# Turning the experts' rows in a mixture-of-experts stage: TensorE transposes against DMA transposes of 16-bit halves

## The chip, the cores and the metric

The kernel runs on one core of a Trainium2 chip. The metric is the device time of one execution in microseconds; the median of the runs is used. The profile comes from one more execution, taken by the hardware profiler. PE is TensorE (matrix products; PEld is its weight load), ACT is ScalarE, DVE is VectorE, POOL is GpSimd and SP is SyncE, which here only issues DMAs.

## The reference

Four steps run one after the other on 2048 tokens (8 x 256) of width 256: an attention by autocorrelation, a feed-forward step with eight experts of 256 tokens each, a cross attention with 16 heads, and a mixture of experts with two experts for each token beside a shared expert. Each step reads the layer norm of `x` and is added to it. The change touches the last step:

```python
x = x + _L1_ffn_ref(_layernorm(x, axis=-1), gate_W, w1_e, w3_e, w2_e, w1_s, w3_s, w2_s)

def _L1_ffn_ref(hidden_states, gate_W, w1_e, w3_e, w2_e, w1_s, w3_s, w2_s):
    flat = hidden_states.reshape(-1, d)
    probs = jax.nn.softmax((flat @ gate_W.T).astype(jnp.float32), axis=-1)
    top_v, top_i = jax.lax.top_k(probs, 2)
    gates = jnp.zeros((T, e), probs.dtype).at[jnp.arange(T)[:, None], top_i].set(top_v)
    g = jax.nn.silu(jnp.einsum('td,edf->etf', flat, w1_e))
    u = jnp.einsum('td,edf->etf', flat, w3_e)
    out_e = jnp.einsum('etf,efd->etd', g * u, w2_e)
    routed = jnp.einsum('te,etd->td', gates, out_e)
    ...   # shared: the same form with w1_s, w3_s, w2_s
    return 0.5 * shared + 0.5 * routed
```

Everything is float32, with inner width F = 1024 and E = 8 experts.

## The kernel before

**The sparse form.** Only the chosen pairs of token and expert are computed. The router writes each token's row (256 normed values, eight gates, the token's number: ROW = 265 floats) into a buffer `Td` in memory, where every expert has its own range. `load_rows(e)` (L3489) reads an expert's first 512 rows into the tile `R`, [128, 4, 265], by one DMA on SyncE's queue (530 KB); there is one such buffer. The few rows beyond 512 are handled in 32-row slots by the generator `slots()` (L3598), a step at a time beside the blocks, with its own weight loads (`sab`, `sc`, L3593).

**Turning.** Products need the model width on the partitions, but `R` has the tokens there. `Turned` (L3497) turns the rows: `half(kc)` makes four TensorE transposes of 128x128 into a PSUM tile `pt` (L3509) and one ScalarE copy of the 512 columns to `RT` (L3512). The first half also copies the token numbers and gates out of `R` (L3514, L3515, VectorE). Two halves make an expert's `RT`, [128, 2, 512].

**Blocks and units.** The stage's main part is a loop over NBLK = 11 blocks b of 512 rows each: 0 and 1 for the shared expert, 2 to 9 for the eight experts, 10 for the shared expert again. A block is four up units (b, 0) to (b, 3), each giving 2 x 128 of the 1024 inner columns of both w1 and w3, and one down unit. The down unit of block b - 1 stands between (b, 0) and (b, 1). Each unit computes its 2x2 block product with seven partial products in place of eight. Sums of operands are formed ahead by VectorE: `UpWeights.steps` (L3105) for the weights, into `HP`, `DownWeights.steps` (L3134) into rows of `X`, `Rows.steps` (L3159) for the turned rows, into `T` and `RT`. All of these sums are lines L3083, which is a helper.

**The order inside a unit** is written out by hand in `run_unit` (L3407), and engines work in the order in which it emits:

```python
u.mm(u.a, A11, "b11", True); u.seed()            # ACT copies a to B
if before is not None: before.silu_2()           # ACT, previous unit
u.mm(u.e, S1, "t1", True);   u.read_p5()         # ACT reads e
end_open()                                       # previous unit's last product, gate, sums
for do in early: do()
u.mm(u.a, S2, "t2");         u.read_u2()         # ACT reads a
u.mm(u.b, A12, "b21")
for do in amid: do()
u.mm(u.e, S4, "b22");        u.read_c12()        # DVE
for do in late: do()
u.mm(u.a, S3, "t3");         u.read_c22()        # DVE
for do in after: do()
```

`seed` is L3222, `read_p5` L3245 and `read_u2` L3249. In a down unit `read_u2` is two scaled copies to the output rows `Y` (L3353). PSUM tiles `a` and `e` come in pairs; S2 writes over the `a` that seed reads, and S3 over the `a` that `read_u2` reads. The products of up units are L3234, those of down units L3293. In the lists `early`, `amid`, `late` and `after` the block loop (L3796) puts side work. The two halves of an expert's turning go to `early` and `amid` of the down unit in the block before the expert's own, its row sums to `late`. For the first expert they go to unit (1, 3), with the sums after it.

**SyncE's queue.** DMAs are issued in program order; one that waits holds back all behind it. In a block these are the next expert's `wab` (2 x 1 MB, after (b, 0), L2916), `R` (after the down unit), `wc` (1 MB, after (b, 1), L2926), and, in blocks 3 to 6, the slots' `sab` and `sc`, emitted in (b, 3). `Od` in memory collects the output; GpSimd adds each expert's rows to it by scattering DMAs (`add_rows`, L3517).

`HP` (16 x 265 floats for each partition) held the routed rows earlier; in this part its first 3072 floats hold weight sums. `X` holds the residual; its rows 0 to 5 are reused for the down weights' sums, and its last four rows lie in `Od` until block 10 fetches them back.

Of the kernel before, what the change touches and what calls it, by code (L numbers as in the profile page):

```python
# [8 lines left out]

F32 = mybir.dt.float32  # L10
BF16 = mybir.dt.bfloat16
U32 = mybir.dt.uint32
I32 = mybir.dt.int32
AF = mybir.ActivationFunctionType
ALU = mybir.AluOpType
# [4 lines left out]
P = 128  # L20
LN_EPS = 1e-5
CAP1 = 576
FIRST = 512
# [1063 lines left out]
def fast_path(  # L1087
# [33 lines left out]
    nc = tc.nc  # L1121
    B, S, D = x.shape
    T = B * S
    NT = T // P
    KC = D // P
    TPB = S // P
    E = L0_ffn_w1.shape[0]
# [22 lines left out]
    X = res.tile([P, NT, D], F32, name="X")  # L1150
# [3 lines left out]
    ROW = D + E + 1  # L1154
# [13 lines left out]
    ident = const.tile([P, P], F32, name="ident")  # L1168
# [93 lines left out]
    pm = l0.enter_context(tc.tile_pool(name="pm", bufs=2))  # L1262
# [34 lines left out]
    for dst, src, i in (  # L1297
# [12 lines left out]
        out=bqd.rearrange("o (b c) -> (o b) c", b=B),  # L1310
        in_=L0_xattn_bq.partition_broadcast(B),
    )
    nc.scalar.dma_start(
        out=WZ[:, :, DH : 2 * DH],
        in_=L0_xattn_Wq.rearrange("(kc p) c -> p kc c", p=P),
# [267 lines left out]
    for h in range(TPB):  # L1583
# [36 lines left out]
        out=tri,  # L1620
        in_=tri,
# [26 lines left out]
    for sign, base in ((1, 1), (-1, 16)):  # L1648
        nc.gpsimd.affine_select(
            out=rows_f,  # L1650
            in_=rows_f,
# [33 lines left out]
    for r in range(2):  # L1685
        (nc.sync if r == 0 else nc.scalar).dma_start(
            out=Gd[0, 0 : S * W2].rearrange(
                "(tt p r w) -> p tt r w", p=P, r=2, w=S
            )[:, :, r, :],
            in_=G,  # L1690
# [4 lines left out]
        out=DG,  # L1695
        in_=Gd[0, :].rearrange("(tt p w) -> p tt w", p=P, w=W2 + 1)[:, :, 1 : S + 1],
# [53 lines left out]
    for tt in range(2):  # L1750
# [3 lines left out]
    rest = pa.tile([P, S], F32, name="rest")  # L1754
# [4 lines left out]
        out=rest, in_to_replace=top[:, 0, :], in_values=pcorr, imm_value=-3.0e38  # L1759
# [16 lines left out]
        out=Wd[:, 0:W2].rearrange("o (r s) -> o r s", r=2),  # L1776
        in_=wrow.unsqueeze(1).to_broadcast([P, 2, S]),
# [4 lines left out]
        out=CW,  # L1782
        in_=bass.AP(wd.tensor, wd.offset + P - 1, [[WD - 1, P], [P, 2], [1, S]]),
# [186 lines left out]
    sums = pa.tile([P, NT, 2], F32, name="sums")  # L1970
# [50 lines left out]
    halves = [slice(m * S, (m + 1) * S) for m in range(2)]  # L2021
# [7 lines left out]
    b = order_b  # L2029
# [101 lines left out]
    def load_row(e):  # L2131
# [14 lines left out]
        out=Yd.rearrange("(c p) d -> p c d", p=P),  # L2146
        in_=blank[:, 0:D].unsqueeze(1).to_broadcast([P, NT, D]),
# [300 lines left out]
    for e in range(E - 1):  # L2448
        if e == 5:

            wpv = L1_xattn_Wp.rearrange("(c g m d) n -> m g d c n", c=NB, g=4, m=2)
            for m in range(2):
                for g in range(4):
# [3 lines left out]
                        out=bvc[r0 : r0 + DH, :],  # L2457
                        in_=bkv[:, 1, :].rearrange("(c g m) d -> m g d c", c=NB, g=4)[m, g],
# [70 lines left out]
    ps_m = banks.enter_context(tc.tile_pool(name="ps_m", bufs=3, space=PSUM))  # L2529
# [436 lines left out]
    for b in range(B):  # L2966
        for c in range(NB):
# [55 lines left out]
            if prev is None:  # L3023
# [12 lines left out]
                HP = pg1.tile([P, NT, ROW], F32, name="HP")  # L3036
# [20 lines left out]
    FULL = FIRST // P  # L3057
# [7 lines left out]
    lrows = slice(LAST * (TB // P), NT)  # L3065
    HT2 = TB // 2
    HF = F // 2
# [17 lines left out]
    class UpWeights:  # L3085


        def __init__(self, wab, sums, s1=None):
            self.sums = sums
            self.raw = {  # L3090
                (h, kc): wab[:, :, kc, h * HF : (h + 1) * HF]
                for h in range(2)
                for kc in range(KC)
            }
            self.part = {
                A11: self.raw[0, 0],
                A12: self.raw[0, 1],
                A22: self.raw[1, 1],
                S1: self.raw[1, 0] if s1 is None else s1,
                S3: sums[:, :, 0],  # L3100
                S2: sums[:, :, 1],
                S4: sums[:, :, 2],
            }
# [120 lines left out]
    class Up(Unit):  # L3224
        n = TB
# [56 lines left out]
    class Down(Unit):  # L3282
        n = HT2
# [123 lines left out]
    def run_unit(u, early=(), amid=(), late=(), after=()):  # L3407

        before = open_unit[0]
        u.mm(u.a, A11, "b11", True)  # L3410
        u.seed()
        if before is not None:
            before.silu_2()
        u.mm(u.e, S1, "t1", True)
        u.read_p5()
        end_open()
        for do in early:
            do()
        u.mm(u.a, S2, "t2")
        u.read_u2()  # L3420
        u.mm(u.b, A12, "b21")
        for do in amid:
            do()
        u.mm(u.e, S4, "b22")
        u.read_c12()
        for do in late:
            do()
        u.mm(u.a, S3, "t3")
        u.read_c22()
        for do in after:  # L3430
            do()
        open_unit[0] = u
# [56 lines left out]
    def load_rows(e):  # L3489
        R = pe2.tile([P, FULL, ROW], F32, tag="R", name="R", bufs=1)  # L3490
        nc.sync.dma_start(
            out=R,
            in_=Td[e * CAP1 : e * CAP1 + FIRST, :].rearrange("(r p) w -> p r w", p=P),
        )
        return R

    class Turned:  # L3497


        def __init__(self, e, R):  # L3500
            self.e, self.R = e, R
            self.RT = pe2.tile([P, KC, FIRST], F32, tag="RT", name="RT")
            self.ids = pe2.tile([P, FULL], U32, tag="ids", name="ids", bufs=3)
            self.gates = pe2.tile([P, FULL], F32, tag="gts", name="gts", bufs=3)

        def half(self, kc):
            pt = ps_m.tile([P, FULL, P], F32, tag="pm", name="pt")
            for r in range(FULL):
                nc.tensor.transpose(  # L3509
                    pt[:, r, :], self.R[:, r, kc * P : (kc + 1) * P], ident  # L3510
                )
            nc.scalar.copy(self.RT[:, kc, :], pt.rearrange("p r q -> p (r q)"))  # L3512
            if kc == 0:
                nc.vector.tensor_copy(self.ids, self.R[:, :, ROW - 1])  # L3514
                nc.vector.tensor_copy(self.gates, self.R[:, :, D + self.e])  # L3515

    def add_rows(Y, ids):  # L3517
        nc.gpsimd.indirect_dma_start(  # L3518
# [164 lines left out]
    pe2 = ctx.enter_context(tc.tile_pool(name="pe2", bufs=2))  # L3683
# [63 lines left out]
    ps_m = ctx.enter_context(tc.tile_pool(name="ps_m", bufs=1, space=PSUM))  # L3747
# [23 lines left out]
    turned = {}  # L3771

    def up_unit(b, k):
        u = Up(ups[b], xs_[b], k, acts.setdefault(b, []))
        u.with_sums = b < NBLK - 1
        return u

    def down_unit(b):
        if b < 2:
            return SharedDown(downs[b], acts.pop(b), b + 1)  # L3780
        t = turned.pop(b)
        return RoutedDown(downs[b], acts.pop(b), t.gates, t.ids)
# [13 lines left out]
    for b in range(NBLK):  # L3796


        n = b + 1
        rest = ups[b].steps(P, HF) if b >= 2 else []  # L3800
        run_unit(up_unit(b, 0), after=rest[:2])
        if b == 0:
            Rs[2] = load_rows(0)
        if b >= 2 and b - 1 < E:
            W_up[b - 1] = load_up(w1p, b - 1)
        halves = []
        if 2 <= n < NBLK - 1:
            t = turned[n] = Turned(n - 2, Rs.pop(n))
            xs_[n] = Rows(t.RT)
            halves = [lambda: t.half(0), lambda: t.half(1)]  # L3810
        sums = xs_[n].steps() if n < NBLK else []
        if b > 0:
            late = b == 1
            run_unit(
                down_unit(b - 1),
                early=([] if late else halves[:1]) + rest[2:],
                amid=[] if late else halves[1:],
                late=[] if late else sums,
            )
        if 2 <= b < E:  # L3820
            Rs[b + 2] = load_rows(b)
        for k in range(1, NK):
            early, amid, after = [], [], []
            if k == 1 and 2 <= n < NBLK:
                ups[n] = UpWeights(WS[0] if n == NBLK - 1 else W_up.pop(n - 2), SW)
                after = ups[n].steps(0, P)
            if 2 <= b < NBLK - 1:
                if k == 2:
                    downs[b] = DownWeights(W_down.pop(b - 2), TW)
                    after = downs[b].steps()[:2]  # L3830
                if k == 3:
                    after = downs[b].steps()[2:]
            if b == 0:
                after = ([assign_slots], sums, shared_down.steps())[k - 1]
            if b == 1 and k == 3:
                early, amid, after = halves[:1], halves[1:], sums
            run_unit(up_unit(b, k), early, amid, after=after)
            if k == 1:
                if b >= 2 and b - 1 < E:
                    W_down[b - 1] = load_down(w1p, b - 1)  # L3840
                if b == 1:
                    flags()
                    experts = slot_experts()
                if b == 2:
                    beside = slots()
                if b == NBLK - 1:
                    nc.sync.dma_start(out=X[:, lrows, :], in_=odv[:, lrows, :])
                    nc.sync.dma_start(
                        out=out.rearrange("b s d -> (b s) d")[0 : LAST * TB, :],
                        in_=Od[0 : LAST * TB, :],  # L3850
                    )
            if beside is not None and (b, k) != (2, 2):
                next(beside, None)
        if b == 1:
            Rs[3] = load_rows(1)
    last_down(WS[1], acts.pop(NBLK - 1))
    order.close()

# [51 lines left out]
```

## Time and profile before

| | |
|---|---|
| median of 3 runs | 832.65 us (831.88 to 832.73) |
| the profiled execution | 830.43 us, of it 828.7 us from first to last instruction |
| granted TensorE clock | 0.998 |
| transposes of the experts' rows (L3509) | 64, from 452.3 to 711.7 us |
| their copies on ScalarE (L3512) | 16, 585 ns each |
| one steady block | 41.0 us |
| TensorE busy from 430 to 828 us | 392.4 of 398 us |
| ScalarE busy from 430 to 828 us | 143.4 of 398 us |

The page of a profile lists, in parts, each engine's busy time, the span in slices, the DMA queues, the chain of work that ended last, the costliest groups of instructions and the DMA issues. In a group's line stand the source line, engine, operation, output and inputs, shapes and count; then busy us, mean ns of one, and the engine's idle time ahead of them with what ended it. In the timeline a line gives the start in us, the duration from the first start to the last end, engine, line, operation and how many were merged; a bracket is idle time before it and what it waited for. "SPq" is SyncE's queue.

### The profile page before, as it was taken

The page shows a single profiled execution, that of the slowest core. Times are in us where ns is not written, and L with a number is a line of the kernel's source. Part 1 is how long each engine was busy: PE and PEld are TensorE (multiplying, and loading weights), DVE is VectorE, ACT ScalarE, POOL GpSimd, SP SyncE. Part 2 cuts the span into 40 slices and gives each one's busy share as a digit, 9 for nine tenths or more (in the row PEclk, how much of TensorE's full clock was granted, in tenths as well). Part 3 has the DMA queues.
Part 4 walks back from the last instruction along what each step waited for, and adds up shares of the span by engine and source line. Part 5 has one row for each costly group of instructions (what it writes and reads, how often), then busy time and mean ns, then how long its engine had stood idle before and what let it go on. Part 6 is the DMA issues. An engine that isn't in the chain of part 4 may idle for free.

```text
span 828.7 us, 13872 instructions
## 1 busy us (share of the span) xinstructions
PE 806.3 (97%) x5188; PEld 636.2 (77%) x5188; DVE 522.3 (63%) x1470; ACT 348.7 (42%) x720; POOL 216.8 (26%) x293
## 2 busy tenths in 40 slices
PE   7999999999999999999999999999999999999997
PEld 6546787778745555557898989797979798999996
DVE  6377877440456586555775866767676758586731
ACT  4344454324377777431333233333333433443430
POOL 6251131230125455452330000202111232112020
PEclk9999999999999999999999999999999999999999
DMA  8395567942160000042120474656575754311023
GB/s 261 97 277 177 178 207 224 297 158 84 51 178 15 14 1 28 34 168 89 67 67 26 142 242 135 190 168 187 172 199 161 201 167 122 105 13 20 8 35 124
DMA packets 87316, 105.40 MB, mean 127 GB/s; under 512 B 9000, under 2 KB 77832, under 8 KB 87208
## 3 DMA queue, kind: packets, MB, share of 16 engines
q1 hardware_dynamic: 78568, 91.10, 35.0%
q0 software_dynamic: 7920, 13.02, 7.2%
q8 instruction: 43, 0.70, 0.4%
q10 hardware_dynamic: 752, 0.30, 0.1%
q14 instruction: 33, 0.27, 0.1%
HBM read 80.61 MB, written 25.37 MB: 128 GB/s over the span
## 4 chain that ended last, share of the span: by engine, by line
PE 88%; DMA 5%; DVE 3%; POOL 2%; ACT 1%; issue 1%; ACTq 0%; SPq 0%; DVEq 0%; POOLq 0%
PE a L3234 18%; PE e L3234 9%; PE a L3293 9%; PE py L2389 6%; PE ph L2372 5%; PE B L3234 5%; PE e L3293 4%; PE p L2652 4%; PE py L3439 3%; PE pv L2667 3%; PE B L3293 2%; PE pp L2718 2%; DMA R<-NMd,ids 2%; PE pgt L3196 2%; PE pp L2619 2%; PE pu L3196 2%
## 5 line engine op out<-in xcount | busy, mean ns | idle before, releaser
L3518 POOL DMA_INDIRECT Od<-Y,ids x32 | 51.6, 1612 | 300.5 <-DVE T L3083 184.0
L3222 ACT COPY B<-a 128x512 f32<-128x512 f32 (+1 forms) x54 | 28.6, 531 | 180.5 <-PE a L3234 142.6
L2660 ACT ACTIVATE ex<-p,scale 128x512 f32<-128x512 f32 x128 | 77.2, 689 | 27.5 <-PE p L2652 26.3
L3234 PE MATMUL a<-T,HP 128*128 128x256 f32 x288 | 73.9, 379 | 0.0
L3083 DVE TENSOR_TENSOR cc<-e,s 128x512 f32<-128x512 f32 x44 | 30.4, 691 | 58.0 <-PE e L3234 58.0
L3234 PE MATMUL a<-RT,wab 128*128 128x256 f32 x256 | 66.6, 383 | 0.0
L3083 DVE TENSOR_TENSOR act<-act 128x256 f32<-128x256 f32 (+1 forms) x120 | 61.4, 512 | 2.7
L2372 PE MATMUL ph<-RT,w 128*128 128x256 f32 x256 | 61.7, 389 | 0.8 <-ACT RT L2359 0.7
L2389 PE MATMUL py<-w,A 128*128 128x256 f32 x256 | 61.6, 388 | 0.0
L3234 PEld LDWEIGHTS a<-T,HP 128*128 128x128 f32 x288 | 54.0, 190 | 7.0
L3234 PEld LDWEIGHTS a<-RT,wab 128*128 128x128 f32 x256 | 46.4, 190 | 8.4 <-issue 1.6
L2381 ACT ACTIVATE A<-ph,b1c 128x256 f32<-128x256 f32 x64 | 30.0, 472 | 53.9 <-PE ph L2372 50.6
L2372 PEld LDWEIGHTS ph<-RT,w 128*128 128x128 f32 x256 | 45.3, 190 | 8.9 <-ACT A L2381 1.1
L2389 PEld LDWEIGHTS py<-w,A 128*128 128x128 f32 x256 | 46.6, 190 | 6.4
L2892 POOL DMA_INDIRECT Td<-HP,to x32 | 32.9, 1030 | 56.9 <-DMA Td<-HP,to 51.6
L2652 PE MATMUL p<-QM,KT 32*128 32x512 f32 x256 | 43.4, 640 | 0.4 <-DVE QM L2633 0.4
L3083 DVE TENSOR_TENSOR act<-act,cc 128x512 f32<-128x512 f32 x44 | 30.4, 691 | 17.6 <-ACT act L3268 17.1
L2399 POOL DMA_INDIRECT Yd<-Y,ids x16 | 15.7, 984 | 81.9 <-DVE Y L2398 49.0
L2667 PE MATMUL pv<-ex,VA 128*32 128x256 f32 x512 | 34.5, 385 | 0.2 <-DVE ov L2677 0.2
L3249 ACT COPY s<-a 128x512 f32<-128x512 f32 x44 | 25.7, 585 | 20.4 <-PE a L3234 20.4
L2667 PEld LDWEIGHTS pv<-ex,VA 128*32 128x32 f32 x512 | 13.5, 109 | 27.0 <-issue 11.7
L3234 PE MATMUL e<-T,wab 128*128 128x256 f32 x128 | 33.0, 380 | 0.3 <-DVE T L3083 0.3
(525 smaller groups left out, 1745.0 us busy)
## 6 DMA issues: line engine op xcount, KB each, us to landing
w<-in_L_ffn_w_dram SPq DMA_DIRECT2D x16, 1024.0 KB, 6.0
wab<-in_L_ffn_w_e_dram SPq DMA_DIRECT2D x16, 1024.0 KB, 4.9
wc<-in_L_ffn_w_e_dram SPq DMA_DIRECT2D x8, 1024.0 KB, 5.4
sab<-in_L_ffn_w_e_dram SPq DMA_DIRECT2D x32, 256.0 KB, 2.9
R<-Td SPq DMA_DIRECT2D x8, 530.0 KB, 3.7
sc<-in_L_ffn_w_e_dram SPq DMA_DIRECT2D x16, 256.0 KB, 2.8
Td<-blank SPq DMA_DIRECT2D x2, 1590.0 KB, 10.2
X<-in_x_dram SPq DMA_DIRECT2D x4, 512.0 KB, 5.3
```

Of the source, the lines that this page charges most:

```text
L2372: nc.tensor.matmul(ph, w1[:, kc, f * P : (f + 1) * P], RT[:, kc, :], start=(kc == 0), stop=(kc == KC - 1),)
L2381: nc.scalar.activation(A[:, f, :], ph, AF.Gelu_apprx_tanh, bias=b1c[:, e, f : f + 1])
L2389: nc.tensor.matmul(py, A[:, f, r * P : (r + 1) * P], w2[:, f, :], start=(f == 0), stop=(f == NF - 1),)
L2652: nc.tensor.matmul(ps[g].rearrange("p m q -> p (m q)"), KT[rows, c, k0 : k0 + P], QM[b][rows, c].rearrange("p m q -> p (m q)"), start=True ...
L2660: nc.scalar.activation(e4[:, g], ps[g], AF.Exp, scale=scale)
L2667: nc.tensor.matmul(pvs[b, c][32 * g : 32 * g + 32, m, :], VA[:, b * TPB + kt, 8 * c + 2 * g + m, :], ex[b, c, kt][:, g, m, :], start=(kt = ...
L2892: nc.gpsimd.indirect_dma_start(out=Td, out_offset=bass.IndirectOffsetOnAxis(ap=to[g][:, k, j : j + 1], axis=0), in_=HP[:, GT * g + j, :], ...
L3083: eng.tensor_tensor(out, a, b, op)
L3196: nc.tensor.matmul(ps, wab[:, m, kc, fs], xs[kc], start=(kc == 0), stop=(kc == KC - 1),)
L3234: nc.tensor.matmul(ps[:, m * HT2 : (m + 1) * HT2], self.w.get(m, left, self.k), self.x.part[right], start=start and m == 0, stop=True, ski ...
L3293: nc.tensor.matmul(ps[:, qs], self.acts[k][:, left, qs], self.w.get(right, k), start=start and i == 0 and k == 0, stop=(k == NK - 1), skip ...
L3518: nc.gpsimd.indirect_dma_start(out=Od, out_offset=bass.IndirectOffsetOnAxis(ap=ids, axis=0), in_=Y, in_offset=None, compute_op=ALU.add,)
```

## The change

The experts' rows are turned by DMA. A float32 is taken as two 16-bit halves, since the DMA transpose that is used moves 16-bit elements. `take_apart(i)` (ScalarE, two of the four groups of rows) copies the halves of `R` apart into a part of `X` that is idle then, low halves first, and issues two DMA transposes on SyncE's queue, of [128, 512] 16-bit elements each, into the unused end of `HP`. `join(kc)` (ScalarE) puts two turned halves together again into `RT`. The copies are of 16-bit integers, so the bits arrive unchanged.

Token numbers and gates are copied when `Turned` is made; their buffers are four in place of three. For expert b (of block b + 2), `take_apart` stands in `amid` of unit (b, 3), two blocks ahead of use, and `join` in `early` of the down unit in the block ahead. The first expert's `take_apart` stands in (1, 1), its `join` in (1, 3); the second's in (2, 0) and (2, 1), its sums in `late` of (2, 2). `load_rows(1)` moves from the end of block 1 to (1, 1).

```diff
     class Turned:
         def __init__(self, e, R):
-            self.e, self.R = e, R
+            self.ids = pe2.tile([P, FULL], U32, tag="ids", name="ids", bufs=4)
+            self.gates = pe2.tile([P, FULL], F32, tag="gts", name="gts", bufs=4)
+            nc.vector.tensor_copy(self.ids, R[:, :, ROW - 1])
+            nc.vector.tensor_copy(self.gates, R[:, :, D + e])
+            self.R = R
             self.RT = pe2.tile([P, KC, FIRST], F32, tag="RT", name="RT")
-            self.ids = pe2.tile([P, FULL], U32, tag="ids", name="ids", bufs=3)
-            self.gates = pe2.tile([P, FULL], F32, tag="gts", name="gts", bufs=3)
-
-        def half(self, kc):
-            pt = ps_m.tile([P, FULL, P], F32, tag="pm", name="pt")
-            for r in range(FULL):
-                nc.tensor.transpose(
-                    pt[:, r, :], self.R[:, r, kc * P : (kc + 1) * P], ident
-                )
-            nc.scalar.copy(self.RT[:, kc, :], pt.rearrange("p r q -> p (r q)"))
-            if kc == 0:
-                nc.vector.tensor_copy(self.ids, self.R[:, :, ROW - 1])
-                nc.vector.tensor_copy(self.gates, self.R[:, :, D + self.e])
+            self.parts = X[:, lrows, :].bitcast(U16)
+            self.turned = (
+                HP.rearrange("p n r -> p (n r)")[:, 2 * 3 * HF : 2 * 3 * HF + KC * FIRST]
+                .bitcast(U16)
+                .rearrange("p (c q) -> p c q", q=FIRST)
+            )
+
+        def take_apart(self, i):
+            two = slice(2 * i, 2 * i + 2)
+            nc.scalar.copy(
+                self.parts[:, two].rearrange("p r (t d) -> p r t d", t=2),
+                self.R[:, two, 0:D].bitcast(U16).rearrange("p r (d t) -> p r t d", t=2),
+            )
+            for r in (2 * i, 2 * i + 1):
+                nc.sync.dma_start_transpose(
+                    out=self.turned[:, :, r * P : (r + 1) * P],
+                    in_=self.parts[:, r],
+                )
+
+        def join(self, kc):
+            nc.scalar.copy(
+                self.RT[:, kc, :].bitcast(U16).rearrange("p (q t) -> p q t", t=2),
+                self.turned[:, kc : kc + 3 : 2, :].rearrange("p t q -> p q t"),
+            )
...
-        run_unit(up_unit(b, 0), after=rest[:2])
+        amid = []
+        if b == 2:
+            t = turned[n] = Turned(n - 2, Rs.pop(n))
+            amid = [lambda: t.take_apart(0), lambda: t.take_apart(1)]
+        run_unit(up_unit(b, 0), amid=amid, after=rest[:2])
...
-        halves = []
+        joins = []
         if 2 <= n < NBLK - 1:
-            t = turned[n] = Turned(n - 2, Rs.pop(n))
-            xs_[n] = Rows(t.RT)
-            halves = [lambda: t.half(0), lambda: t.half(1)]
-        sums = xs_[n].steps() if n < NBLK else []
+            t = turned[n] if n > 2 else None
+            if n > 3:
+                joins = [lambda: t.join(0), lambda: t.join(1)]
+                xs_[n] = Rows(t.RT)
+        sums = xs_[n].steps() if n in xs_ else []
         if b > 0:
-            late = b == 1
-            run_unit(
-                down_unit(b - 1),
-                early=([] if late else halves[:1]) + rest[2:],
-                amid=[] if late else halves[1:],
-                late=[] if late else sums,
-            )
+            run_unit(down_unit(b - 1), early=rest[2:] + joins, late=sums)
...
+            if b == 1 and k == 1 or 2 <= b < E and k == 3:
+                m = n if k == 1 else n + 1
+                v = turned[m] = Turned(m - 2, Rs.pop(m))
+                amid = [lambda: v.take_apart(0), lambda: v.take_apart(1)]
             if b == 1 and k == 3:
-                early, amid, after = halves[:1], halves[1:], sums
-            run_unit(up_unit(b, k), early, amid, after=after)
+                t = turned[n]
+                early, amid = [lambda: t.join(0)], [lambda: t.join(1)]
+                xs_[n] = Rows(t.RT)
+                after = xs_[n].steps()
+            if b == 2 and k == 1:
+                amid = [lambda: t.join(0), lambda: t.join(1)]
+                xs_[n] = Rows(t.RT)
+            if b == 2 and k == 2:
+                late = xs_[n].steps()
+            run_unit(up_unit(b, k), early, amid, late, after)
+            if b == 1 and k == 1:
+                Rs[3] = load_rows(1)
...
-        if b == 1:
-            Rs[3] = load_rows(1)
```

More of the change, by code (lines that the diff above doesn't have):

```diff
@@ L11 @@
 BF16 = mybir.dt.bfloat16
-U32 = mybir.dt.uint32
+U32, U16 = mybir.dt.uint32, mybir.dt.uint16
 I32 = mybir.dt.int32
@@ L3822, in fast_path @@
         for k in range(1, NK):
-            early, amid, after = [], [], []
+            early, amid, late, after = [], [], [], []
             if k == 1 and 2 <= n < NBLK:
```

## The prediction

> **What bounds the kernel now.** I read the page first: busy times, then the chain that ended last.
>
> ```profile
> PE 806.3 (97%) x5188; PEld 636.2 (77%) x5188; DVE 522.3 (63%) x1470; ACT 348.7 (42%) x720; POOL 216.8 (26%) x293
> PE 88%; DMA 5%; DVE 3%; POOL 2%; ACT 1%; issue 1%; ACTq 0%; SPq 0%; DVEq 0%; POOLq 0%
> ```
>
> TensorE is busy 97% of the span and is 88% of the chain; ScalarE has more than half its time free. So an instruction taken from TensorE shortens the run by what it occupies there, if nothing takes the gap. Second, the groups of instructions by shape, for the transposes that go and their copies:
>
> ```profile
> L3509 PE MATMUL pt<-ident,R 128*128 128x128 f32 x64 | 9.6, 273 | 0.0
> L3512 ACT COPY RT<-pt 128x512 f32<-128x512 f32 x16 | 9.4, 585 | 14.1 <-PE pt L3509 13.7
> ```
>
> 273 ns is one transpose from start to end; they are pipelined, so it isn't its price. Third, the timeline of TensorE around one group:
>
> ```profile
> 589.93 1.95 PE L3293 MATMUL B<-wc,act 128*128 128x128 f32 x16
> 591.72 0.60 PE L3509 MATMUL pt<-ident,R 128*128 128x128 f32 x4
> 592.16 1.95 PE L3293 MATMUL e<-wc,act 128*128 128x128 f32 x16
> ```
>
> Sixteen products take 1.79 us from start to start (589.93 to 591.72). The four transposes hold the next group back by 592.16 - 591.72 = 0.44 us, 110 ns each, and no line shows an idle bracket. The other fifteen groups give 0.43 or 0.44 us too. Fourth, ScalarE in the unit before the down unit of the same block, and then in that down unit:
>
> ```profile
> 572.79 0.41 ACT L3259 ACTIVATE act<-a 128x256 f32<-128x256 f32 x1
> 573.64 0.58 ACT L3249 COPY s<-a 128x512 f32<-128x512 f32 x1 [0.44 <-PE a L3234]
> 578.29 0.57 ACT L3222 COPY B<-a 128x512 f32<-128x512 f32 x1 [4.07 <-PE a L3234]
> 587.91 0.38 ACT L3259 ACTIVATE act<-a 128x256 f32<-128x256 f32 x1 [0.24 <-PE a L3234]
> 588.35 0.58 ACT L3512 COPY RT<-pt 128x512 f32<-128x512 f32 x1
> 590.13 0.62 ACT L3353 ACTIVATE Y<-a,gts 128x128 f32<-128x128 f32 x2 [1.20 <-PE a L3293]
> ```
>
> After read_u2 (L3249) ScalarE waits 4.07 us for the next unit's first product; elsewhere in the stage this gap is 2.87 to 3.1 us. Last, SyncE's queue over one block, where the weight loads are issued:
>
> ```profile
> 563.75 4.66 SPq L3593 DMA_DIRECT2D sab<-in_L_ffn_w_e_dram  x8
> 577.26 2.45 SPq L3593 DMA_DIRECT2D sc<-in_L_ffn_w_e_dram  x4
> 580.01 0.89 SPq L2916 DMA_DIRECT2D wab<-in_L_ffn_w_e_dram  x2
> 592.35 0.37 SPq L3491 DMA_DIRECT2D R<-Td  x1
> 599.44 0.37 SPq L2926 DMA_DIRECT2D wc<-in_L_ffn_w_e_dram  x1
> 604.79 4.39 SPq L3593 DMA_DIRECT2D sab<-in_L_ffn_w_e_dram  x8
> ```
>
> A block is 41.04 us (604.79 - 563.75) and its loads are 2 + 1 + 2 + 0.5 + 1 = 6.5 MB.
>
> **What the skill says.** "TensorE: Matmul & The Clock Gate", Part 4: PE-mode transpose, gives about 275 ns for a transpose in a kernel's context. The trace agrees (273 ns), but that is a latency; the spacing, 110 ns, is what is saved. "ScalarE: Activation LUTs", What ACT_TABLE_LOAD costs: 0.833 ns an element, fp32 and bf16 alike. The trace agrees for f32: L3222 takes 570 ns for 512 columns and 357 for 256, (570 - 357) / 256 = 0.83. It shows no strided 16-bit copy. For DMA transposes the skill has two prices, far apart, and the trace has none. "DMA: Bandwidth & Descriptors", Latency and other measured facts: an effective 261 GB/s. "VectorE: DVE Perf Modes", The three transpose paths: 1309 ns for one 128x128 block of 16 bits.
>
> **Removed.** 64 transposes, 16 groups x 0.44 = 7.0 us of TensorE. They lie in L3234/L3293 work that runs without a gap, so all of it comes off the end. ScalarE loses 16 x 0.585 = 9.4 us, which nobody waited for.
>
> **Added on ScalarE.** Each expert gets two take_apart copies and two join copies of 1024 elements. One costs 585 + 512 x 0.83 = 1.01 us; a source in SBUF adds about 0.05 (L3268 takes 633), so I take 1.05. 32 x 1.05 = 33.6 us, net +24 us; ScalarE goes from 349 to about 373 us of some 822 and stays far from a bound. What matters is place:
> - take_apart stands behind read_u2. The pair ends at 574.22 + 2.10 = 576.3; the next seed can't start before 578.29. In the tightest units the gap is 2.87 us, still 0.7 more than needed. A late seed has a further 1.0 us before its reader waits (seed ends 571.62, the product that overwrites its source starts 572.58). Cost 0.
> - join stands behind the gate that ends at 588.29: 588.3 to 590.4. Behind it wait the two Y copies (590.13 now; then 590.4 to 591.0). The product that overwrites their source comes at 593.94 now, 593.06 without the two groups. 2.0 us to spare. Cost 0.
> - Bounds: not below nothing, as none of this was on the chain. Above, if strided 16-bit elements take twice as long, the join pair ends at 592.5 and Y at 593.1, 0.1 us late, and the take_apart pair (4.2 us) overruns a 2.87 gap by 1.3, 0.3 beyond its spare: 8 x 0.4 = 3 us.
> - At the first expert join(0) stands ahead of read_u2 of (1,3): 453.2 to 454.25, read_u2 to 454.83, its reader at 455.13. It just fits, and the sums behind it, which now cost 0.42 us (first product of (2,0) at 456.86, second at 458.14, not 457.72), are neither earlier nor later by more than 0.3. Cost 0.
>
> **Added on DMA.** Four transposes of 128 KB for each expert, on SyncE's queue behind take_apart's halves (575.3 and 576.3). At 261 GB/s one is 0.5 us, an estimate from that page (131,072 bytes); the shortest landing on this queue is 1.8 us (ids_s, 0.1 KB), so four have landed some 5 us after the first is issued, near 581. At 1.309 us for a block and no overlap, one (four blocks) is 5.2 us and four are 21 us, an estimate from the other page. I take the low end: the moved loads of that stretch reach 371 to 416 GB/s (windows of 2 us, 584 to 588), while 1309 ns for a lone 32 KB block is mostly the landing time that even 0.1 KB pays. join wants them at 588.3 (window 13 us from 575.3), and TensorE waits only if they are later than 590.3.
>
> **Moved on SyncE.** In the built program's order the transposes stand ahead of the eight sab loads, and they wait for ScalarE. So sab goes from 563.75 to about 577.5; sc follows at 582, wab at 585 (580.01 now), then R and wc. From 577 the queue owes 0.5 + 2 + 1 + 2 = 5.5 MB. The stretch 578 to 590 moved 3.15 MB in 12 us, 262 GB/s, so 21 us: done at 598. Their readers are pgu at 602.7 and the sums HP<-wab at 603.51: 5 us to spare, which hides this at no cost; without cover each microsecond late would come six times. R can land earlier than before, since take_apart frees its buffer in (b,3), not in the next block's down unit; its reader moves earlier too, to about 610, and it lands near 600. The ids and gates copies (0.16 us each on VectorE) only move, and a fourth pair of buffers lets them. R(3) is now issued in block 1 behind four transposes, wab of the second expert at about 464 instead of 457, with its reader at about 485. Cost 0.
>
> **The sum.** 830.43 (the profiled execution; its span is 828.7) - 7.0 = 823.4. The median of the runs is 832.65, 2.2 above it; the same difference gives 825.6.
>
> **Rivals.**
> - Slow transposes (ends slower). Mechanism: the four in a row take the queue longer than join's window, and join holds ScalarE, which holds the Y copies and TensorE. It decides from 3.8 us a transpose: at 15.2 us the steady experts lose 0.3 us each (575.4 + 15.2 + 2.1 + 0.6 = 593.3 against 593.06) and the first, whose window is only 443.1 to 453.5, loses 4.8; 6 x 0.3 + 4.8 = 6.6, and the gain is gone (832.2). At 5.24 us: steady 599.1 - 593.06 = 6.0, x 6 = 36; first 464.1 - 453.5 = 10.6; 825.6 + 47 = 873. For it: the 1309 ns, and that no trace here shows a transpose. Against: above.
> - Slow 16-bit copies: 825.6 + 3 = 828.7. For it: strides are untried here. Against: the skill's one rate for both widths.
> - The weights come late although the transposes are quick: the 5 us are used up if the rate from 577 on falls under 5.5 / 26 = 210 GB/s. At 180 (the mean of 577 to 604) wab is 4 us late, of which VectorE's slack hides some 2: six blocks x 2 = 12, 837. Against: that mean has idle stretches (0 GB/s at 590).
> - That the change doesn't act: the built order has 64 transposes fewer on TensorE, so no chance.
>
> **Chances.** As worked 0.76 (824.3 to 827); slow copies 0.07; transposes near the deciding point, no change, 0.04; slow transposes 0.09; late weights 0.04. About 0.2% (1.7 us) is what a measurement here can tell from no change: faster 0.83, same 0.04, slower 0.13. The range takes the likeliest case and the slow copies: 823.8 to 829.2.
>
> **What would show it.** No L3509 lines, L3234 and L3293 groups back to back, TensorE busy about 799. take_apart and join near 1.05 us; next seeds still waiting for TensorE. The landing time of the transposes under 10 us. "ACT RT <- DMA" waits in the list would be the slow rival; "DVE HP <- DMA wab" the late weights. A block (sab to sab) should take 41.04 - 0.88 = 40.2 us. A landing over 13 us or a copy over 2 us makes the prediction wrong.

## The result, and the profile after

The changed kernel takes 827.5 us (median of 15 runs, 825.08 to 832.95) against 832.94 us for the kernel before on the same chip (15 runs, 831.11 to 836.42). The ratio is 0.9933, 95% interval 0.9914 to 0.9952. The profiled execution took 825.11 us, with a span of 823.4 us, against 830.43 and 828.7 before.

First, from the page of the changed kernel, the busy times, and from the groups by shape the new copies (busy us, mean ns of one, idle time ahead of them):

```profile
PE 800.0 (97%) x5124; PEld 630.1 (77%) x5124; DVE 521.6 (63%) x1470; ACT 371.9 (45%) x736; POOL 217.1 (26%) x293
```

```profile
L3529 ACT COPY RT<-HP 128x1024 uint16<-128x1024 uint16 x16 | 17.9, 1162 | 0.0
L3518 ACT COPY X<-R 128x1024 uint16<-128x1024 uint16 x16 | 16.0, 1051 | 0.0
```

TensorE has 64 instructions and 6.3 us less, ScalarE 16 instructions and 23.2 us more. The last column is what matters: neither `join` (L3529) nor `take_apart` (L3518) waited for anything, so no transpose landed too late for `join`. Line numbers behind L3500 have moved; the transposes' issue is L3523, the slots' loads are L3610.

Second, the timeline of TensorE in the down unit that the prediction showed:

```profile
585.85 1.95 PE L3293 MATMUL a<-X,act 128*128 128x128 f32 x16
587.63 1.95 PE L3293 MATMUL B<-wc,act 128*128 128x128 f32 x16
589.42 1.95 PE L3293 MATMUL e<-wc,act 128*128 128x128 f32 x16
591.21 1.95 PE L3293 MATMUL a<-X,act 128*128 128x128 f32 x16
```

The starts lie 1.78 or 1.79 us apart. The two steps of 0.44 us that stood between such groups are gone, with no bracket in their place.

Third, ScalarE in the same block:

```profile
571.78 0.59 ACT L3249 COPY s<-a 128x512 f32<-128x512 f32 x1 [0.44 <-PE a L3234]
572.26 2.00 ACT L3518 COPY X<-R 128x1024 uint16<-128x1024 uint16 x2
576.43 0.57 ACT L3222 COPY B<-a 128x512 f32<-128x512 f32 x1 [2.17 <-PE a L3234]
...
586.33 2.21 ACT L3529 COPY RT<-HP 128x1024 uint16<-128x1024 uint16 x2
588.44 0.63 ACT L3353 ACTIVATE Y<-a,gts 128x128 f32<-128x128 f32 x2
```

The `take_apart` pair fills 2.00 us of the gap behind `read_u2`; 2.17 us of it are still idle ahead of the next seed. The `join` pair puts the Y copies back to 588.44; they end at 589.07, 2.1 us ahead of the product at 591.21 that overwrites their source.

Fourth, SyncE's queue in the same block:

```profile
573.34 5.12 SPq L3523 DMA_TRANSPOSE HP<-X  x4
578.71 5.61 SPq L3610 DMA_DIRECT2D sab<-in_L_ffn_w_e_dram  x8
584.58 2.11 SPq L3610 DMA_DIRECT2D sc<-in_L_ffn_w_e_dram  x4
586.80 1.16 SPq L2916 DMA_DIRECT2D wab<-in_L_ffn_w_e_dram  x2
588.35 0.37 SPq L3491 DMA_DIRECT2D R<-Td  x1
```

The order is as foretold, but the four transposes hold the queue for 5.12 us by themselves (the median of one is 1.25 us). From the sab of the block before (538.60) to this one a block takes 40.11 us.

Last, a wait that is new. TensorE and then VectorE in unit (2,2):

```profile
488.93 1.03 PE L3234 MATMUL e<-T,wab 128*128 128x256 f32 x4
490.40 1.13 PE L3234 MATMUL a<-RT,wab 128*128 128x256 f32 x4 [0.45 <-DVE cc L3083]
```

```profile
487.47 0.69 DVE L3083 TENSOR_TENSOR cc<-e,s 128x512 f32<-128x512 f32 x1 [0.19 <-PE e L3234]
488.08 0.75 DVE L3083 TENSOR_TENSOR T<-RT 128x256 f32<-128x256 f32 x2
488.86 0.43 DVE L3083 TENSOR_TENSOR T<-RT,T 128x256 f32<-128x256 f32 x1
489.32 0.42 DVE L3083 TENSOR_TENSOR RT<-RT,T 128x256 f32<-128x256 f32 x1
489.67 0.68 DVE L3083 TENSOR_TENSOR cc<-a,s 128x512 f32<-128x512 f32 x1
```

The second expert's row sums (four operations in the three `T<-RT` and `RT<-RT` lines, put in `late`) stand between `read_c12` (487.47) and `read_c22` (489.67). TensorE's next product, due 0.87 us after 488.93, needs the tile that `read_c22` reads, and starts 0.6 us late.

**A finer measure than the median.** Runs of one kernel differ by up to 8 us, while some of the edits below move less than one. All these kernels share everything up to the routing, so I take the length of the changed stage: from the start of the product `B<-tri,ones_b` of the routing to the start of the last group of the last down product. In the changed kernel's timeline of TensorE:

```profile
395.94 0.59 PE L3768 MATMUL B<-tri,ones_b 128*128 128x512 bf16 x2
...
805.86 11.39 PE L3439 MATMUL py<-wc_-1_6532,act 128*128 128x256 f32 x52
```

That is 409.92 us. Read in the same way:

| kernel | stage, us | against before |
|---|---|---|
| before | 416.16 | |
| after | 409.92 | -6.24 |
| after_again (the same kernel) | 409.92 | -6.24 |
| sab_ahead | 409.92 | -6.24 |
| no_turn | 409.21 | -6.95 |
| sums_after | 409.21 | -6.95 |
| both | 409.22 | -6.94 |
| twice | 413.79 | -2.37 |
| acts_twice | 415.16 | -1.00 |
| join_early | 431.67 | +15.51 |

The same kernel gives the same stage to 0.01 us in two executions (after and after_again) whose spans differ by 5 us (823.4 and 828.4). So differences of some tenths can be read here. Of the 6.24 us the profiled executions show 5.3: the stage began 0.87 us later (395.94 against 395.07), in work that the change doesn't touch. In the medians 5.4 us come off; the interval of the ratio, 4.0 to 7.2 us, holds both figures.

### The profile page after: what moved, and what is told of

The parts are those of the page before. It is cut to its first block, busy times and chain, and to the rows that moved or that the text cites. A ratio compares the mean times of both kernels' runs of the same rounds, so it can differ in the third digit from the quotient of the medians.

```text
span 823.4 us, 13830 instructions
## 1 busy us (share of the span) xinstructions
PE 800.0 (97%) x5124; PEld 630.1 (77%) x5124; DVE 521.6 (63%) x1470; ACT 371.9 (45%) x736; POOL 217.1 (26%) x293
## 2 busy tenths in 40 slices
DMA packets 104724, 109.59 MB, mean 133 GB/s; under 512 B 26408, under 2 KB 95240, under 8 KB 104616
## 5 line engine op out<-in xcount | busy, mean ns | idle before, releaser
L3234 PE MATMUL e<-T,wab 128*128 128x256 f32 x128 | 32.9, 380 | 0.3 <-DVE T L3083 0.3
```

The costliest lines, as they stand in the source:

```text
L3234: nc.tensor.matmul(ps[:, m * HT2 : (m + 1) * HT2], self.w.get(m, left, self.k), self.x.part[right], start=start and m == 0, stop=True, ski ...
```

## The experiments

**Theory**: 7.0 us of transposes are gone from TensorE, the rest of the change is hidden, but for the moved sums. **Rivals**: the weights that now stand behind the transposes come late; ScalarE or the transposes cost something that is taken off the gain.

**no_turn**: the kernel before with nothing in the place of the transposes. Its rows are not turned, so its output isn't the reference's; it shows what all of the turning on TensorE cost.

```diff
-            pt = ps_m.tile([P, FULL, P], F32, tag="pm", name="pt")
-            for r in range(FULL):
-                nc.tensor.transpose(
-                    pt[:, r, :], self.R[:, r, kc * P : (kc + 1) * P], ident
-                )
-            nc.scalar.copy(self.RT[:, kc, :], pt.rearrange("p r q -> p (r q)"))
+            nc.scalar.copy(
+                self.RT[:, kc, :].rearrange("p (r q) -> p r q", q=P),
+                self.R[:, :, kc * P : (kc + 1) * P],
+            )
```

> The kernel before, with the 64 TensorE transposes taken out: ScalarE copies the rows from R to RT unturned, so the experts' products are of unturned rows and the result is not the reference's. It measures the removal alone. Theory (a transpose costs its spacing, 16 groups of 0.44 us): 7.0 us less than before, about 826 us, TensorE's units back to back. Rival (the transposes hid other waits, so that less than their spacing comes off): 4 to 5.5 us less, and new idle brackets on TensorE in the experts' blocks.

Measured: 824.63 us (823.26 to 826.99, 4 runs), ratio 0.9919 (0.9892 to 0.9945); the stage is 6.95 us shorter. So 16 x 0.44 = 7.0 us is what the transposes cost, and a change that only takes them off TensorE has no more to give. The rival's new idle brackets don't appear.

**sums_after**: the second expert's sums behind unit (2,2) in place of its `late`.

```diff
-                late = xs_[n].steps()
+                after = after + xs_[n].steps()
```

> The changed kernel, with the second expert's four row sums put behind the last VectorE read of unit (2, 2) in place of ahead of it. The changed kernel's trace shows TensorE waiting 0.45 us, its weight load 0.85 us, for VectorE's second cc sum there. Theory (this moved step is what is missing of the 7.0 us): the wait at about 490 us goes and the run is 0.6 to 0.9 us shorter. Rival (other work hides it, or the wait comes back in the next unit, where the sums then delay the activations): within 0.2 us of the changed kernel.

Measured: 825.49 us (824.27 to 826.87, 6 runs), ratio 0.9924 (0.9904 to 0.9944). The same stretch, VectorE and then TensorE:

```profile
487.72 0.69 DVE L3083 TENSOR_TENSOR cc<-e,s 128x512 f32<-128x512 f32 x1 [0.19 <-PE e L3234]
488.51 0.69 DVE L3083 TENSOR_TENSOR cc<-a,s 128x512 f32<-128x512 f32 x1
```

```profile
489.17 1.03 PE L3234 MATMUL e<-T,wab 128*128 128x256 f32 x4
490.04 1.03 PE L3234 MATMUL a<-RT,wab 128*128 128x256 f32 x4
```

`read_c22` follows at once, the product starts 0.87 us after the one ahead of it, and the stage is 409.21, that of no_turn. So the moved sums cost 0.71 us, and the rest of the change (DMA, ScalarE, SyncE's order) costs nothing that this stage shows.

**sab_ahead**: the slots' up weights are issued a unit earlier, ahead of the transposes.

`load_slots` is split for this into an up part and a down part.

```diff
...
             nc.vector.tensor_tensor(a, a, pgu[:, 1, :], ALU.mult)
+            up = load_slots(q + 1, False) if q + 1 < NQ else load_up(wsp, -1)
             yield
...
-                w = load_slots(q + 1)
+                w = up + load_slots(q + 1, True)
...
-                WS = load_l1(wsp, -1)
+                WS = up, load_down(wsp, -1)
```

> The changed kernel, with the slots' up weights (sab, and the shared expert's after the last of them) issued right behind the products that free their buffer, in (b, 1), so that on SyncE's queue they stand ahead of the DMA transposes, as in the kernel before. The changed kernel's executions spread from 825.1 to 833.0 us, with their lower half within 0.6 us. Theory (late weights: the eight sab loads held back behind the transposes push wab to the edge of its use, and in some executions past it): the upper half goes, median 825.3, nearly all within 826. Rival (the spread comes from the earlier stages, or from the transposes themselves): the same spread, median 827 to 828.

Measured: 825.64 us (824.84 to 827.07, 6 runs), ratio 0.9925 (0.9905 to 0.9945); stage 409.92, the same as after. In SyncE's timeline sab goes ahead of the transposes now, and wab 5.2 us earlier than the 586.80 of after:

```profile
561.99 4.96 SPq L3613 DMA_DIRECT2D sab<-in_L_ffn_w_e_dram  x8
581.59 0.91 SPq L2916 DMA_DIRECT2D wab<-in_L_ffn_w_e_dram  x2
```

Nothing is gained in the stage: the later loads are hidden. The median does lie near the theory's 825.3, but sums_after, run beside it without this edit, has 825.49; so that needn't be the loads' doing, and by the stage the theory falls.

**twice**: experts 2 to 7 have each transpose issued a second time, into rows of `X` that nobody reads then.

```diff
...
+                if self.e >= 2:
+                    nc.sync.dma_start_transpose(
+                        out=self.twice[:, :, r * P : (r + 1) * P],
+                        in_=self.parts[:, r],
+                    )
```

> The changed kernel, with each DMA transpose of experts 2 to 7 issued a second time into idle rows of X that nobody reads. One issue takes 1.25 us on SyncE's queue, so four more push sab, sc and wab back by 5 us in each block. Theory (late weights): wab lands after its first use in the four or five blocks that have slot loads, VectorE's HP sums then wait for a DMA, 2 to 5 us a block: 8 to 20 us over the changed kernel. Rival (there is slack of 5 us and more on the queue): within 2 us of the changed kernel. Rival (the transposes' landing binds): ScalarE's join waits for a DMA, and TensorE behind it.

Measured: 829.54 us (826.29 to 833.07, 20 runs), ratio 0.9969 (0.9955 to 0.9982); stage 3.87 us longer than after. From the list of waits, who waited for what (total us, times, longest):

```profile
DVE HP L3083 <- DMA wab<-in_L_ffn_w_e_dram: 13.9, 4, 3.7
ACT RT L3538 <- DMA HP<-X: 0.2, 1, 0.2
```

Now the next expert's weights do come late, in four blocks. In the block shown above their issue is at 598.13, where the first transpose is at 578.58: 19.55 us, against 586.80 - 573.34 = 13.46 in after. That is 6.1 us later, and the sums wait 3.31 us. So after has some 2.8 us to spare there by the issue, and more by the landing, since the four added transposes also take DMA time (some 0.7 us each, see below). The DMA packets of the traces agree: the last of wab ends at 608.89 here, 0.5 us before the sums begin, and at 596.94 in after, 3.8 us before they begin at 600.77. The prediction had 5 us to spare. `join` waited once, for 0.2 us, with eight transposes ahead of it.

So the theory had the place right and the size wrong: of VectorE's 13.9 us of waiting only 3.87 reach the stage, about 1 us a block, where 2 to 5 were expected; the rest is hidden. TensorE's brackets add up to 2.5 us more than after's; the remaining 1.4 us lies in spacings without a bracket, and I have not followed it further.

**join_early**: the join copies of six experts, to the start of up unit (b+1,0), right behind the transposes, to see when these land. (Counted from 0 these are experts 2 to 7, six pairs of copies; the expectation's "3 to 7" is a slip, its six blocks are right.)

```diff
-        run_unit(up_unit(b, 0), amid=amid, after=rest[:2])
+        first = []
+        if 3 < n < NBLK - 1:
+            first = [lambda: turned[n].join(0), lambda: turned[n].join(1)]
+        run_unit(up_unit(b, 0), early=first, amid=amid, after=rest[:2])
...
-                joins = [lambda: t.join(0), lambda: t.join(1)]
```

> The changed kernel with the two join copies of experts 3 to 7 moved a unit forward, to the start of up unit (b+1,0), right behind the last DMA transpose: it exposes when the transposes land, which the list of issues doesn't show. Last transpose issued at about 578.5 us. Theory (one transpose is some 0.7 us of the DMA engines and lands about 2 us after its issue): ScalarE's first join waits for a DMA into HP until about 580 to 581, and TensorE loses 1 to 3 us in each of six blocks: 832 to 844. Rival (transposes are slow, and only the 10 us ahead of join hide that): the wait lasts until 585 to 588, 7 us and more in each block: 868 or later. If they land before their queue is free again: no wait for a DMA, and 826 to 830.

Measured: 849.21 us in one run, the stage 21.75 us longer than after, 3.6 for each of the six: beyond the upper end of what I expected, for a reason that follows. SyncE's queue, ScalarE and TensorE in one block:

```profile
581.20 5.12 SPq L3523 DMA_TRANSPOSE HP<-X  x4
```

```profile
588.77 2.21 ACT L3529 COPY RT<-HP 128x1024 uint16<-128x1024 uint16 x2 [2.33 <-DMA HP<-X]
590.89 0.58 ACT L3249 COPY s<-a 128x512 f32<-128x512 f32 x1
```

```profile
591.52 1.13 PE L3234 MATMUL a<-T,HP 128*128 128x256 f32 x4 [2.95 <-ACT s L3249]
```

The last of the four has landed by 588.77: 7.6 us after the first is issued, 2.4 us after the queue is done with the last. In after's time that is 573.34 + 7.57 = 580.9 (in its trace the last packet of these four ends at 580.42), and `join` comes at 586.33: 5.4 us to spare. The slow price, which would need 21 us, is out.

TensorE's brackets of 1.8 to 3.2 us sum to 15.4; the other 6 us are mostly its clock, the share of full speed that the throttle grants (PEclk). Windows of 2 us around another of these waits (length, PE busy, instructions, PEclk, DMA share, GB/s):

```profile
632.00:634.00 2.00, 0.00 (x0) 1.00 0.94 320
634.00:636.00 2.00, 1.74 (x5) 0.66 0.72 228
636.00:638.00 2.00, 2.00 (x12) 0.50 0.96 292
638.00:640.00 2.00, 2.00 (x19) 0.99 1.00 325
```

After a pause of 2.3 us the granted clock is 0.50 from 634.62 to 638.03, for 3.41 us, and 12 products take the time of 19. Three of the six pauses go with such a stretch (those of 2.31, 2.40 and 3.15 us), and each stretch costs up to 1.7 us. Three don't (those of 1.76, 2.87 and 2.95 us), so the length of the pause alone doesn't decide.

What the three have in common shows when the trace is cut into windows of 3.41 us that end where the clock falls (634.62, 679.00, 719.96; the starts lie whole multiples of 3.41 us apart). In the window just ahead of each fall TensorE is busy for 1.10, 1.01 and 0.78 us. The pause of 2.95 us lies across two windows of this grid (from 586.84 and from 590.25), with 1.73 and 2.14 us busy; those of 2.87 and 1.76 us leave 1.58 us and more. So in this stage the idle time within one window of a fixed grid tells the two kinds apart. One execution of one kernel shows it, and earlier in the program the border is less clear: 1.95 us busy stand ahead of a fall in twice, 1.51 ahead of none in acts_twice.

**acts_twice**: every take_apart and join copy is made twice.

```diff
-            nc.scalar.copy(
+            for _ in range(2):
+                nc.scalar.copy(
...
```

> The changed kernel with every take_apart and every join copy of ScalarE made twice: 32 copies more, 16 x 1.05 + 16 x 1.16 = 35 us more of ScalarE. Theory (the copies lie in gaps with about 1 to 2 us of spare for a pair): the steady take_apart pair grows from 2.0 to some 4.1 us and ends near 576.4, where the next seed starts at 576.43 in the profile of the changed kernel; the join pair ends 2.3 us later, against 2.0 us of spare; so at most 0.4 us for each of six to eight experts, up to 3 us in all: 825.5 to 828.7. Rival (ScalarE has less cover than I read, because read_u2, the gates and the Y copies are needed sooner): 1.5 us and more for each expert, 838 or later, with TensorE waiting for ACT B, s or Y in each block. If nothing at all is hidden: 825.6 + 35 = 861.

Measured: 832.04 us (829.83 to 835.73, 12 runs), ratio 0.9988 (0.9973 to 1.0003); the stage is 5.24 us longer than after, for 32.9 us more of busy ScalarE (404.8 against 371.9). ScalarE and then TensorE in the block:

```profile
579.23 4.17 ACT L3519 COPY X<-R 128x1024 uint16<-128x1024 uint16 x4
583.39 0.57 ACT L3222 COPY B<-a 128x512 f32<-128x512 f32 x1
...
593.29 4.61 ACT L3531 COPY RT<-HP 128x1024 uint16<-128x1024 uint16 x4
597.81 0.62 ACT L3353 ACTIVATE Y<-a,gts 128x128 f32<-128x128 f32 x2
```

```profile
596.38 1.95 PE L3293 MATMUL e<-wc,act 128*128 128x128 f32 x16
598.48 1.72 PE L3293 MATMUL a<-X,act 128*128 128x128 f32 x13
```

The seed now follows the copies without a gap, and the last product of the down unit starts 2.10 us after the one ahead of it, not 1.79: a wait of 0.3 us for the Y copies that carries no bracket. From take_apart to take_apart a steady block takes 40.56 us (579.23 to 619.79) against 40.16 (572.26 to 612.42): 0.40. The first and second expert lose 1.2 us each (take_apart of the second comes 4.86 us later than in after, where that of the first came 3.67 later; the third, 6.06). So the copies as they are lie hidden, and doubled they are out of cover by just that much. The theory's 3 us was too low mainly for these two experts.

**after_again and both**: the changed kernel once more, beside the kernel with the edits of sums_after and sab_ahead together.

> The changed kernel itself, once more, beside the three variants. Theory: 7.0 us of transposes removed, 0.7 us given back where the sums of the second expert stand ahead of VectorE's read_c in unit (2,2), and a spread between executions that comes from an earlier stage: a median between 825.0 and 828 us, ratio to the kernel before between 0.991 and 0.994, and in its profile a bracket of some 0.5 us on VectorE's cc near 490 us. Rival (the change itself makes its time unsteady): a median of 827.5 or more, while the variants stay near 825.5.

> The changed kernel with the sums of the second expert behind unit (2,2) and the slots' up weights issued a unit earlier, ahead of the DMA transposes. Theory: only the first of the two edits has anything to give, 0.7 us; so 0.7 us below the changed kernel run beside it, about 825, with a stage of 409.2 us from the product B<-tri,ones_b to the last down group. Rival (the two delays cover each other, so that each alone shows less than both): more than 1.2 us below the changed kernel, a stage under 408.7 us.

Measured: after_again 827.2 us (825.68 to 830.48, 6 runs), ratio 0.9934 (0.991 to 0.9959); both 827.24 us (824.76 to 829.55, 6 runs), ratio 0.9935 (0.9912 to 0.9958). The stage of `both` is 409.22 us, 0.70 less than the 409.92 of after_again beside it, as the theory has it, and the rival (under 408.7) falls. In the medians the 0.7 us can't be seen: two kernels with a stage of 409.92 gave 825.64 and 827.2, two with 409.21 or 409.22 gave 825.49 and 827.24. The lower of each pair ran on one chip and the higher on another, so the chip may be part of what lies between them.

In the profiled executions what hides it is an earlier part of the kernel: their stages begin anywhere from 395.07 (before) to 401.14 (after_again), and none of these differences arises later than 220 us. In the profile of twice, and then in that of the kernel before, TensorE's first waits of the search (a product of counts, L2183), and windows of 2 us (length, PE, PEld, DVE, ACT, POOL busy, PEclk, DMA share, GB/s):

```profile
74.51 0.21 PE L2183 MATMUL pcn<-B32h,cnt 128*128 128x32 f16 x1 [2.69 <-DVE above L2166]
```

```profile
74.00:76.00 2.00, 1.49 (x5) 1.23 (x6) 1.70 (x9) 0.20 (x1) 0.00 (x0) 0.50 0.99 312
76.00:78.00 2.00, 2.00 (x8) 1.50 (x7) 0.71 (x5) 0.54 (x2) 0.00 (x0) 0.65 0.38 139
```

```profile
72.39 0.19 PE L2183 MATMUL pcn<-B32h,cnt 128*128 128x32 f16 x1 [0.90 <-DVE above L2166]
```

```profile
74.00:76.00 2.00, 2.00 (x10) 1.51 (x11) 1.83 (x11) 0.74 (x2) 0.00 (x0) 1.00 0.56 186
76.00:78.00 2.00, 2.00 (x11) 1.49 (x10) 1.86 (x9) 0.74 (x2) 0.00 (x0) 1.00 0.27 98
```

Where that wait is longer (2.69 against 0.90 us), the clock falls to half behind it, and this execution is 3.4 us late by the next such products. In after_again the clock dips twice further on (0.84 from 95 to 105 us, 0.83 from 175 to 185), and its stage begins at 401.14 in place of 395.94. The clock isn't all of it: the stage of acts_twice begins at 399.60 without a dip in the search. These are single executions; that the spread of all runs comes from there is likely, not shown. The Trainium skill, "TensorE: Matmul & The Clock Gate", Part 1: The HAM clock gate, has the array's clock gated to half after an idle window of about 3.4 us; the half clock agrees (0.50), but here windows of 3.41 us in which TensorE was busy for 0.78 to 1.10 us had it follow, so an idle time of 2.3 us can be enough.

## Why the prediction was right, and where it was off

**The transposes removed: right.** Worked out at 7.0 us, measured as 6.95 by no_turn, from the spacing of 110 ns and not the 273 ns of a transposition's length (64 x 0.273 would have been 17.5 us).

**ScalarE: right in place, small errors of size.** take_apart takes 1.05 us as estimated; join takes 1.16, not 1.05. The rate of 0.83 ns, read from f32 copies, gives 0.85 us for 1024 elements, and the fixed part of those copies is 0.14 (570 ns less 512 x 0.83); strides and a source in SBUF thus add 0.06 and 0.17 us. Both pairs are covered. The rival of slow copies was priced at 8 x 0.4 = 3 us; acts_twice has 5.2. The 0.4 of a steady expert is met (0.40), but the first two experts have less cover, which the rival left out, and lose 1.2 each.

**The DMA transposes: right between the two prices, with a term left out.** The price of 0.5 us was a price of DMA engines. The page shows it by queue (packets, MB, share of 16 engines' span), before and after:

```profile
q1 hardware_dynamic: 78568, 91.10, 35.0%
q1 hardware_dynamic: 95976, 95.30, 38.0%
```

That is 38.0% of 823.4 us, against 35.0% of 828.7, so 22.9 us more for 32 transposes, some 0.7 us each (184 GB/s against the 261 of the Trainium skill, "DMA: Bandwidth & Descriptors", Latency and other measured facts). What I left out is that an issue holds SyncE's own queue for 1.25 us. So the four had landed 7.6 us after the first issue, not some 5; the window was 13. The 1309 ns of the Trainium skill, "VectorE: DVE Perf Modes", The three transpose paths, for a 128x128 block isn't the time of such a block within a larger transpose, four of which cost these 1.25 us of queue and 0.7 us of engines.

**SyncE's order: right in order and outcome, late in time.** Against take_apart, which the prediction had at 574.22 and the trace has at 572.26, sab was to come 3.3 us later (577.5) and wab 10.8 (585); they come 6.45 and 14.54 later. The 3.2 and 3.8 us more are for the most part the issue time of 1.25 us a transpose. They used up part of the 5 us to spare: sab_ahead gains nothing, and twice, with 6.1 us more, waits for wab, so about 3 us were left. That the term left out cost nothing is owed to a spare that was counted without it, and so in part to luck. The rival of late weights had the right place and the wrong price: in twice four blocks wait and not six, and lose about 1 us each and not 2.

**First expert: right.** TensorE's wait for its sums is 0.34 us against 0.25 before; no_turn, without any of the DMAs, has 0.34 too.

**The step that failed: what isn't in the sum.** The change puts the second expert's sums in `late` of (2,2). The prediction costs the first expert's sums and not these. What it asks of ScalarE's copies (what stands behind them, and who waits for that) it didn't ask here, of the sums between `read_c12` and `read_c22` on VectorE. They cost 0.71 us. The sums of the later experts stand in `late` of a down unit, and no bracket of TensorE follows them there.

**The sum.** For the profiled execution 823.4 us was foretold, and 825.11 measured: 0.71 from these sums and 0.87 from the later start of the stage are 1.6 of the 1.7. For the median 825.6 was foretold, and 827.5 measured; 0.7 of the 1.9 are the sums, and the rest is within what medians of kernels with one stage length differ by (825.64 and 827.2 above). "What would show it" came as written: TensorE 800.0 us (799), blocks of 40.11 to 40.16 us (40.2), the copies, no wait for `HP` or `wab`.

## What to carry to other kernels

On an engine that is busy 97% of the time, price an instruction that goes by the spacing it causes, and then ask of every instruction that is moved, on every engine, which pair it now stands between: the one loss here came from four vector operations that were moved, not from the new DMAs. Price a DMA three times: its share of the DMA engines, its landing, and how long its issue holds the queue for what stands behind it. When a change is worth less than the spread between executions, compare the length of the changed stage in the traces.

## What the runs showed of the hardware

- A DMA transpose of [128, 512] 16-bit elements within SBUF holds SyncE's queue for 1.25 us (median of 32), where a plain load of 1 MB holds it for 0.37 (wc) or 0.46 us (wab), both medians. Packets under 512 B rise from 9000 to 26408, 544 for each transpose.
- Four in a row have all landed 7.6 us after the first is issued, beside weight loads (join_early); in after the last packet of four ends 5.9 to 7.1 us after the first issue.
- ScalarE copies 1024 16-bit elements with strides in 1.05 us (apart) and 1.16 us (together).
- A TensorE pause of 2.3 us can be followed by half the clock for 3.41 us, so that the pause costs up to 1.7 us more, while one of 2.95 us was not followed so. In join_early's stage the falls follow windows of 3.41 us, on a fixed grid, with 1.10 us of TensorE work or less, and none follows a window with 1.58 us or more.
